# Decay terms through DRAM: thirteen transfers a chunk become eight, and two of the spreads move ahead of the scans

## The chip, the core and the metric

The kernel runs on one core of one Trainium2 chip. A core has five engines that run side by side and meet at semaphores: TensorE (PE; its weight loads are shown apart, as PEld), VectorE (DVE), ScalarE (ACT), GpSimd (POOL) and SyncE (SP), which issues DMAs. ACT and POOL issue DMAs too. The metric is device time in microseconds of one launch.

## The reference

Three layers follow each other on a hidden state of 8 sequences x 1024 tokens x 256, in float32: half a step of a mixture of 8 experts, a "memory" layer, and half a step of the experts again. The change lies in the memory layer:

```python
x = x + 0.5 * ffn(layernorm(x), gate_w, w1, w2)
x = x + attn(layernorm(x), ...)
x = x + 0.5 * ffn(layernorm(x), gate_w, w1, w2)
```

The memory of a sequence is two 64x64 matrices W1, W2 with a momentum S beside them. The tokens go in chunks of 128. The gradient g of a chunk's tokens is taken at the state with which the chunk began, clipped by its norm, and then the state runs token by token:

```python
alpha = (sigmoid(hidden @ aW.T + ab) * 0.1).mean(-1)
eta = (sigmoid(hidden @ eW.T + eb) * 0.9 + 0.05).mean(-1)
theta = (softplus(hidden @ tW.T + tb) * LR).mean(-1)

def step(carry, xs):                      # one token
    Sm, Wm = carry
    gt, et, tt, at = xs
    Sm = et[:, None] * Sm - tt[:, None] * gt
    Wm = (1.0 - at[:, None]) * Wm + Sm
    return ((Sm, Wm), Wm)
```

Each token's output is read from the state after that token: h = silu(q W1), then h W2, an output projection, a norm and a gate.

The kernel does not run this recurrence token by token. With a = 1 - alpha, the state after token t is a sum of three parts: the old W times A(t), the old S times B(t), and the chunk's gradients, each with a weight C(t, s). A is the running product of a, M the running product of eta, and B(t) = a(t) B(t-1) + M(t). C is a 128x128 matrix for each sequence. These are the decay terms that the change is about.

## The kernel before

The 8 sequences are worked on together, chunk by chunk (`NC` = 8 chunks of `P` = 128 tokens, `B` = 8 sequences in `NP` = 4 pairs; of a pair, one sequence lies on partitions 0 to 63 and the other on 64 to 127). The class `Memory` has one small method for each step of a chunk.

The order of the work is written out by hand. `ORDER` (line 1233) is a list of words, and `attention` (line 1248) goes through it once per turn. A word such as `spread` calls that step for the chunk of this turn; `abh1-1` calls `abh` with n=1 for the chunk before, `load1+1` for the chunk after. A step that yields is taken up again at its next word. So each turn mixes steps of up to five chunks, and every engine runs its instructions in the order in which the words issue them. Pools and semaphores are handled by a tile framework: a step that needs another engine's result waits for it in its engine's own queue, and what is behind it there waits too.

The steps around the change, with their lines:

- `ae`, `aem` (693, 708): PE and ACT compute the means. `sig` then holds four rows of 512 numbers: a and eta of sequences 0 to 3 on partitions 0 and 32, of sequences 4 to 7 on partitions 64 and 96.
- `few` (718): four DMAs on SP's queue bring those rows into the small tile `few`, 8 partitions (one for a sequence) x 5 rows x 128: a in row 3, eta in row 4.
- `prods` (732): three scans on DVE over `few`: A into row 0, M into row 2, B into row 1. In the trace all scans have the helper's line, L730.
- `cut` (738): a memset on POOL sets the first token of a and eta to zero, in the small tile, after the scans. `abh1-1` comes next on POOL.
- `spread` (741): on SP, `few` is written to a DRAM tile `kept`; then eta and a go to all 128 partitions (each 128 x 1024 numbers), A and B to `ab`, and the last M to `last`, in six smaller transfers.
- `lt` (756) and `ct` (760): two large scans on DVE, 128 x 1024, over eta and over a. The zero in each sequence's first token is what separates the 8 sequences of one scan. `lt` writes its result over eta. `ends` (765) copies last columns, on POOL.
- `kept` and `past` (796, 788): small copies on POOL for the convolution. (The word `kept` in the order is this step, not the DRAM tile.)
- `abq` (874), `old` (971) and `abh` (1070): POOL multiplies q, the old state and h by A and B. `state` (1001) is the DVE addition that gives the next chunk's state, in the trace L1006.
- `std`, `logits` (1169, 1184): the router of the next layer; POOL's L107 to L112 end in `r_b`, which DVE's L1205 multiplies.
- `xr`, `load` (1100, 658): ACT issues loads of 512 KB each for the residual and for the next chunks.

On SP the thirteen transfers of a chunk are the only ones in this layer, apart from the stores of the last chunk.

Of the kernel before, what the change touches and what calls it, by code (L numbers as in the profile page):

```python
# [10 lines left out]
F32 = mybir.dt.float32  # L11
I32 = mybir.dt.int32
AF = mybir.ActivationFunctionType
ALU = mybir.AluOpType
# [4 lines left out]
P = 128  # L19
B, S, H = 8, 1024, 256  # L20
NT = B * S
NI = NT // P
D = 64
NC = S // P
NP = 4
# [7 lines left out]
class Shared:  # L33
# [95 lines left out]
    def choose(self, pool, dl, mask, ranked=None, cut=lambda ap: ap):  # L129

        nc = self.nc
        n = dl.shape[2]
        full = [P, E, n]
        top = pool.tile([P, 2, n], F32, tag="top", name="top", bufs=1)
        if ranked is None:
            ranked = pool.tile(full, F32, tag="ranked", name="ranked", bufs=1)
        by_e = lambda ap: ap.rearrange("p e i -> p i e")
        nc.vector.tensor_reduce(top[:, 0, :], by_e(dl), AX.X, ALU.max)
        nc.vector.tensor_tensor(dl, dl, top[:, 0:1, :].to_broadcast(full), ALU.subtract)

        nc.vector.scalar_tensor_tensor(
            ranked, dl, -(2.0**-25), self.rank.to_broadcast(full), ALU.is_ge, ALU.mult
        )
        nc.vector.tensor_reduce(top[:, 1, :], by_e(ranked), AX.X, ALU.max)
        first = cut(top[:, 1:2, :])
        nc.vector.tensor_tensor(mask, cut(ranked), first.to_broadcast(list(mask.shape)), ALU.is_equal)


class Slots:
# [37 lines left out]
    def spread(self, _):  # L187

        nc = self.sh.nc
        t_ps = self.pp.tile([P, 512], F32, tag="t", name="t_ps")  # L190
        nc.tensor.transpose(t_ps[:NI, :P], self.by_row, self.sh.ident)
        g = self.pool.tile([NI, P], F32, name="gates")
        nc.scalar.activation(g, t_ps[:NI, :P], AF.Copy, scale=0.5 * 16.0)
        self.gate = self.dr.tile([NT, 1], F32, name="gate_d")
        nc.sync.dma_start(self.gate.rearrange("(i p) o -> i (p o)", p=P), g)
# [310 lines left out]
class Memory:  # L506
# [123 lines left out]
    def new(self, name, shape, **kw):  # L630
        return self.pool.tile(list(shape), F32, tag=name, name=name, **kw)
# [85 lines left out]

    def few(self, c, u, _):

        u.few = self.new("few", (B, 5, P), bufs=1)  # L720
        for h in range(2):
            for n in range(2):
                row = D * h + 32 * n
                self.nc.sync.dma_start(
                    u.few[NP * h : NP * (h + 1), 3 + n, :],
                    u.sig[row : row + 1, 0, :].rearrange("n (j t) -> n j t", j=NP),
                )

    def scan(self, out, m, x, at):
        self.nc.vector.tensor_tensor_scan(out, m, x, at, ALU.mult, ALU.add)  # L730

    def prods(self, c, u, _):
        f = u.few
        self.scan(f[:, 0, :], f[:, 3, :], self.zero, 1.0)
        self.scan(f[:, 2, :], f[:, 4, :], self.zero, 1.0)
        self.scan(f[:, 1, :], f[:, 3, :], f[:, 2, :], 0.0)

    def cut(self, c, u, _):
        self.nc.gpsimd.memset(u.few[:, 3:5, 0:1], 0.0)

    def spread(self, c, u, _):

        nc, new = self.nc, self.new
        kept = self.dram.tile([B, 5, P], F32, tag="kept", name="kept")
        nc.sync.dma_start(kept, u.few)
        u.a, u.eta = new("a", (P, B, P), bufs=1), new("eta", (P, B, P), bufs=1)
        for t, n in ((u.eta, 4), (u.a, 3)):
            nc.sync.dma_start(t, kept[:, n, :].partition_broadcast(P))
        u.ab, u.last = new("ab", (P, 2, NP, P)), new("last", (P, NP, 1))
        for r in range(2):  # L750
            of = kept.rearrange("(p r) n t -> r n p t", r=2)[r]
            for n in range(2):
                nc.sync.dma_start(u.ab[self.half[r], n], of[n].partition_broadcast(D))
            nc.sync.dma_start(u.last[self.half[r]], of[2][:, P - 1 : P].partition_broadcast(D))

    def lt(self, c, u, _):
        flat = lambda ap: ap.rearrange("p b t -> p (b t)")
# [115 lines left out]

    def abq(self, c, u, n):
        self.once(u, "abq", lambda: self.new("abq", (P, 2, NP, P), bufs=1))
        self.nc.gpsimd.tensor_tensor(u.abq[:, n], u.kv[2], u.ab[:, n], ALU.mult)  # L876

# [91 lines left out]
    def old(self, c, u, n):  # L971

        if c + 1 == NC:
            return
        g, st = self.nc.gpsimd, u.st
        at = lambda ap: ap.unsqueeze(3).to_broadcast([P, NP, 2, D])
        self.once(u, "go", lambda: self.new("go", (P, NP, 2, 2, D), bufs=1))
        if n == 0:
            g.tensor_tensor(u.go[:, :, :, 0], st[:, :, :, 0], at(u.ab[:, 0, :, P - 1 : P]), ALU.mult)
        if n == 1:  # L980
            g.tensor_tensor(u.go[:, :, :, 1], st[:, :, :, 1], at(u.ab[:, 1, :, P - 1 : P]), ALU.mult)
        if n == 2:
            g.tensor_tensor(u.go[:, :, :, 0], u.go[:, :, :, 0], u.go[:, :, :, 1], ALU.add)
        if n == 3:
            g.tensor_tensor(u.go[:, :, :, 1], st[:, :, :, 1], at(u.last), ALU.mult)
# [83 lines left out]

    def abh(self, c, u, n):  # L1070
        self.once(u, "abh", lambda: self.new("abh", (P, 2, NP, P), bufs=1))
        self.nc.gpsimd.tensor_tensor(u.abh[:, n], u.hq, u.ab[:, n], ALU.mult)

    def hh(self, c, u, _):
        hh = self.two()
# [160 lines left out]
turn3 turn1 add1-2 load1+1 back_turn0-2 turn2 clip-1 clip-1 lx1+1 turn3 turn2 ae0 back_turn1-2 ae0  # L1236
lx0+1 ae1 lo0-2 old1-1 lo1-2 back_turn0-2 back_turn1-2 ae1 old2-1 old3-1 proj0 clip-1 load0+2 gc0-1
std0-2 gc1-1 aem logits0-2 lx2+1 proj0 proj0 aem logits0-2 hq-1 lx3+1 tap0 tap1 step1-1 logits0-2
few tap2 logits0-2 norm+1 hq-1 hq-1 proj1 step0-1 xr0-1 proj1 prods cut abh1-1 wide1-2 proj1 theta
state-1 wide1-2 tap3 hh-1 proj2 rms1-2 theta tap4 hh-1 xo2-2 abh0-1 theta xn0+1 proj2 zk add2-2  # L1240
proj2 xo3-2 tap5 rh-1 add3-2 zk rows1 soft tap6 rows1 zk softplus lo2-2 pred rows0 lo3-2 pred
back_turn2-2 back_turn2-2 spread tap7 back_turn3-2 rts-1 back_turn3-2 rts-1 ds pred std1-2 tap8
logits1-2 rows0 logits1-2 by_out-1 kept lt logits1-2 ksq sq1 logits1-2 choose1-2 thm pred thm wide0-1 back
past+1 xn1+1 ds by_out-1 abq1 back qk wide0-1 ct back mq0 xn2+1 gate0-1 sq1 store0-2
"""

# [95 lines left out]
```

## Time and profile before

| | us |
|---|---|
| median of three runs | 820.86 (817.55 to 821.42) |
| the profiled execution | 818.81 |
| its span, first to last instruction | 817.0 |
| PE busy | 748.8 (92%) |
| DVE busy | 453.9 (56%) |
| POOL busy | 471.0 (58%) |
| ACT busy | 347.1 (42%) |
| mean granted TensorE clock | 0.948 |

The memory layer lies at about 240 to 580 us; the small scans of its eight chunks begin at 246, 278, 319, 365, 412, 458, 508 and 554 us. Chunks are numbered from 0 here. Ahead of it and behind it are the two expert layers, bound by PE and weights.

In lists in order of time each line gives the start in us, the duration in us, the engine, the source line, the operation, what it writes from what it reads, and in brackets how long the engine had been idle and what ended that. In lists of waits, a line gives who waited, for whom, the total in us, how many times, and the longest. "PEld" is a weight load; it runs ahead of its matmul. A span on POOL includes time in which the operation was held up.

### The profile page before, as it was taken

How to read it: one execution, taken by the hardware profiler on the slowest of the kernel's cores; microseconds unless marked ns; L12 is line 12 of the kernel's file. 1: busy time of each engine (PE TensorE's matmuls, PEld its weight loads, DVE VectorE, ACT ScalarE, POOL GpSimd, SP SyncE). 2: the span in 40 equal slices, each digit the busy share in tenths (PEclk: the TensorE clock that was granted, in tenths of full speed). 3: DMA queues.
4: the chain of work that ended last, by engine and by line, in shares of the span. 5: the costliest groups of instructions: out<-in, count | busy, mean ns of one | idle time of the engine just before them, and what ended most of it. 6: DMA issues, size and time to landing. Idle time of an engine off the chain costs nothing. (4 is left out here: it accounts for less than half of the span.)

```text
span 817.0 us, 13755 instructions
## 1 busy us (share of the span) xinstructions
PE 748.8 (92%) x5256; PEld 544.1 (67%) x5256; DVE 453.9 (56%) x939; ACT 347.1 (42%) x738; POOL 471.0 (58%) x610
## 2 busy tenths in 40 slices
PE   7989999999478999899999999899975899999996
PEld 5657777777336585767767575666763577777775
DVE  7763332220418988788888868978743624322310
ACT  5411222222057676767676655766332122222221
POOL 6626445431234788888888878877754254444411
PEclk9989999999867999999999979999797799999999
DMA  9995445440213334433544532434425724444410
GB/s 299 370 386 166 136 145 168 151 141 16 94 51 80 111 73 125 123 117 79 181 106 155 131 104 80 91 123 99 130 74 183 245 73 139 139 145 139 152 63 18
DMA packets 110945, 110.40 MB, mean 135 GB/s; under 512 B 12384, under 2 KB 103904, under 8 KB 110880
## 3 DMA queue, kind: packets, MB, share of 16 engines
q1 hardware_dynamic: 73312, 66.50, 27.3%
q10 hardware_dynamic: 31680, 31.46, 12.3%
q0 software_dynamic: 5888, 11.57, 4.5%
q8 instruction: 41, 0.67, 0.3%
q14 instruction: 24, 0.20, 0.1%
HBM read 78.80 MB, written 30.64 MB: 134 GB/s over the span
## 5 line engine op out<-in xcount | busy, mean ns | idle before, releaser
L371 ACT ACTIVATE hT<-ph 128x320 f32<-128x320 f32 x128 | 55.9, 437 | 221.9 <-PE ph L364 221.9
L364 PE MATMUL ph<-xT,w1t 128*128 128x320 f32 x512 | 146.0, 438 | 0.9 <-ACT xT L318 0.9
L364 PEld LDWEIGHTS ph<-xT,w1t 128*128 128x128 f32 x512 | 94.7, 190 | 40.6 <-issue 2.7
L392 DVE SCALAR_TENSOR_TENSOR xo<-py,gate,xg 128x256 f32<-128x256 f32 x32 | 15.5, 484 | 186.9 <-PE py L385 186.9
L385 PE MATMUL py<-w2t,hT 128*128 128x256 f32 x512 | 114.6, 382 | 0.0
L385 PEld LDWEIGHTS py<-w2t,hT 128*128 128x128 f32 x512 | 96.1, 190 | 13.7
L287 POOL DMA_INDIRECT gate<-gate_d,get x48 | 45.3, 943 | 39.0 <-DMA gate_d<-gates 25.0
L1111 PE MATMUL pre<-wg,xT 128*128 128x256 f32 x256 | 61.6, 401 | 2.2 <-DVE m L870 2.2
L775 PE MATMUL pre<-xT,w 128*64 128x512 f32 x256 | 61.4, 603 | 0.5 <-ACT kk L807 0.5
L1111 PEld LDWEIGHTS pre<-wg,xT 128*128 128x128 f32 x256 | 50.8, 201 | 11.0 <-DVE m L870 2.7
L1155 POOL TENSOR_TENSOR xo<-xo,xr 128x512 f32<-128x512 f32 x32 | 42.9, 1353 | 20.3 <-DVE xo L1149 20.0
L395 POOL DMA_INDIRECT out<-xo,put x16 | 16.0, 1003 | 54.7 <-DVE xo L392 52.1
L395 POOL DMA_INDIRECT x<-xo,put x16 | 16.0, 1002 | 52.3 <-DVE xo L392 44.4
L678 ACT ACTIVATE xt<-xt,ln_nm,lx_t 128x256 f32<-128x256 f32 x64 | 34.4, 593 | 24.4 <-POOL ln_nm L673 24.4
L1149 DVE SCALAR_TENSOR_TENSOR xo<-tail,rs,gate 128x256 f32<-128x256 f32 x64 | 27.1, 477 | 25.2 <-DMA out<-xo 9.4
L964 DVE TENSOR_TENSOR gc<-ehd,c 128x1536 f32<-128x1536 f32 x16 | 40.0, 2539 | 0.3
L775 PEld LDWEIGHTS pre<-xT,w 128*64 128x64 f32 x256 | 15.8, 136 | 30.4 <-issue 22.4
L685 PE MATMUL pre<-ident,xt 128*128 128x128 f32 x128 | 21.0, 298 | 14.4 <-ACT xt L678 13.0
L876 POOL TENSOR_TENSOR abq<-qq,ab 128x512 f32<-128x512 f32 x16 | 32.8, 2051 | 1.8 <-DMA ab<-kept 1.8
L698 PE MATMUL pre<-xT,w 128*128 128x512 f32 x64 | 32.1, 631 | 0.0
L408 PE MATMUL py<-w2t,hT 128*64 128x128 f32 x512 | 31.5, 276 | 0.0
L276 POOL DMA_INDIRECT xg<-x,get x24 | 23.4, 973 | 13.9 <-DVE get L240 6.8
(254 smaller groups left out, 1593.4 us busy)
## 6 DMA issues: line engine op xcount, KB each, us to landing
w1t<-w_in SPq DMA_DIRECT2D x16, 1024.0 KB
w2t<-w_in SPq DMA_DIRECT2D x16, 1024.0 KB
xt<-hidden_in SPq DMA_DIRECT2D x16, 512.0 KB
x<-xt SPq DMA_DIRECT2D x16, 512.0 KB
xt<-x ACTq DMA_DIRECT2D x16, 512.0 KB
xr<-x ACTq DMA_DIRECT2D x16, 512.0 KB
x<-xo ACTq DMA_DIRECT2D x14, 512.0 KB
out<-xo ACTq DMA_DIRECT2D x14, 512.0 KB
```

The costliest lines, as they stand in the source:

```text
L287: nc.gpsimd.indirect_dma_start(out=gate[:, s : s + 1], out_offset=None, in_=slots.gate, in_offset=bass.IndirectOffsetOnAxis(ap=slots.get[: ...
L364: nc.tensor.matmul(ph[:, :CAP], lhsT=a[:, c, f * P : (f + 1) * P], rhs=at[:, c, :], start=(c == 0), stop=(c == 1),)
L371: nc.scalar.activation(hT[:, f, :], ph[:, :CAP], AF.Relu)
L385: nc.tensor.matmul(py[:, :H], lhsT=hT[:, f, s * P : (s + 1) * P], rhs=b[:, f, :], start=(f == 0), stop=(f == FC - 1),)
L395: nc.gpsimd.indirect_dma_start(out=dst, out_offset=bass.IndirectOffsetOnAxis(ap=slots.put[:, e, s : s + 1], axis=0), in_=xo[:, s, :], in_o ...
L678: self.nc.scalar.activation(x, x, AF.Identity, bias=u.nm[:, j : j + 1], scale=u.r16[:, j : j + 1])
L698: self.nc.tensor.matmul(ps, lhsT=self.w3[:, k, 4 * D : 6 * D], rhs=u.xT[:, k, h * 512 : (h + 1) * 512], start=(k == 0), stop=(k == 1),)
L775: self.nc.tensor.matmul(ps[self.half[r], :], lhsT=self.w3[:, k, f * D : (f + 1) * D], rhs=u.xT[:, k].rearrange("h (p r t) -> h p r t", p=N ...
L876: self.nc.gpsimd.tensor_tensor(u.abq[:, n], u.kv[2], u.ab[:, n], ALU.mult)
L964: self.nc.vector.tensor_tensor(u.gc[:, layer], g.unsqueeze(2).to_broadcast([P, B, 3, D]), u.c3.rearrange("s n j -> s j n").unsqueeze(3).to ...
L1111: self.nc.tensor.matmul(ps[:, q * H : (q + 1) * H], lhsT=u.xT[:, k, j * P : (j + 1) * P], rhs=self.wg[:, k, :], start=(k == 0), stop=(k == 1),
L1155: self.nc.gpsimd.tensor_tensor(u.xo[h][:, two], u.xo[h][:, two], u.xr[h][:, two], ALU.add)
```

## The change

The decay rows go to DRAM first, straight from `sig`, in one transfer of 4 x 512. From there two transfers fill rows 3 and 4 of `few`, and eta and a are spread to 128 partitions at once, before the scans. After the scans only what they made leaves `few`: its rows are so arranged that the last M, A and B are 257 neighbouring numbers of each sequence. They go to a second DRAM tile in one transfer and to `mab` in two. The zero of the first token is now set in the large tiles eta and a, by two memsets in each chunk, and the word `cut` moves in the order from behind `prods` to between `kept` and `lt`. `u.ab` and `u.last` become slices of `mab`, so that A and B have a row step of 257 numbers.

```diff
     def few(self, c, u, _):
+        nc = self.nc
+        kept = self.dram.tile([4, NP * P], F32, tag="kept", name="kept")
+        nc.sync.dma_start(kept, u.sig[0:P:32, 0, :])
+        by_half = kept.rearrange("(h n) x -> n h x", n=2)
         u.few = self.new("few", (B, 5, P), bufs=1)
         for h in range(2):
-            for n in range(2):
-                row = D * h + 32 * n
-                self.nc.sync.dma_start(
-                    u.few[NP * h : NP * (h + 1), 3 + n, :],
-                    u.sig[row : row + 1, 0, :].rearrange("n (j t) -> n j t", j=NP),
-                )
+            nc.sync.dma_start(
+                u.few[NP * h : NP * (h + 1), 3:5, :], by_half[:, h, :].rearrange("n (j t) -> j n t", j=NP)
+            )
+        u.a, u.eta = self.new("a", (P, B, P), bufs=1), self.new("eta", (P, B, P), bufs=1)
+        for to, n in ((u.eta, 1), (u.a, 0)):
+            nc.sync.dma_start(to.rearrange("p (h j) t -> p h (j t)", h=2), by_half[n].partition_broadcast(P))
...
     def prods(self, c, u, _):
         f = u.few
-        self.scan(f[:, 0, :], f[:, 3, :], self.zero, 1.0)
-        self.scan(f[:, 2, :], f[:, 4, :], self.zero, 1.0)
-        self.scan(f[:, 1, :], f[:, 3, :], f[:, 2, :], 0.0)
+        self.scan(f[:, 1, :], f[:, 3, :], self.zero, 1.0)
+        self.scan(f[:, 0, :], f[:, 4, :], self.zero, 1.0)
+        self.scan(f[:, 2, :], f[:, 3, :], f[:, 0, :], 0.0)
+
+    def spread(self, c, u, _):
+        ends = self.dram.tile([B, 2 * P + 1], F32, tag="ends_d", name="ends_d")
+        self.nc.sync.dma_start(ends, u.few.rearrange("b n t -> b (n t)")[:, P - 1 : 3 * P])
+        u.mab = self.new("mab", (P, NP, 2 * P + 1))
+        for r in range(2):
+            of = ends.rearrange("(p r) x -> r p x", r=2)[r]
+            self.nc.sync.dma_start(u.mab[self.half[r]], of.partition_broadcast(D))
+        u.last = u.mab[:, :, 0:1]
+        u.ab = [u.mab[:, :, P * n + 1 : P * (n + 1) + 1] for n in range(2)]

     def cut(self, c, u, _):
-        self.nc.gpsimd.memset(u.few[:, 3:5, 0:1], 0.0)
-
-    def spread(self, c, u, _):
-        nc, new = self.nc, self.new
-        kept = self.dram.tile([B, 5, P], F32, tag="kept", name="kept")
-        nc.sync.dma_start(kept, u.few)
-        u.a, u.eta = new("a", (P, B, P), bufs=1), new("eta", (P, B, P), bufs=1)
-        for t, n in ((u.eta, 4), (u.a, 3)):
-            nc.sync.dma_start(t, kept[:, n, :].partition_broadcast(P))
-        u.ab, u.last = new("ab", (P, 2, NP, P)), new("last", (P, NP, 1))
-        for r in range(2):
-            of = kept.rearrange("(p r) n t -> r n p t", r=2)[r]
-            for n in range(2):
-                nc.sync.dma_start(u.ab[self.half[r], n], of[n].partition_broadcast(D))
-            nc.sync.dma_start(u.last[self.half[r]], of[2][:, P - 1 : P].partition_broadcast(D))
+        for t in (u.eta, u.a):
+            self.nc.gpsimd.memset(t[:, :, 0:1], 0.0)
...
 ORDER
-few tap2 logits0-2 norm+1 hq-1 hq-1 proj1 step0-1 xr0-1 proj1 prods cut abh1-1 wide1-2 proj1 theta
+few tap2 logits0-2 norm+1 hq-1 hq-1 proj1 step0-1 xr0-1 proj1 prods abh1-1 wide1-2 proj1 theta
...
-logits1-2 rows0 logits1-2 by_out-1 kept lt logits1-2 ksq sq1 logits1-2 choose1-2 thm pred thm wide0-1 back
+logits1-2 rows0 logits1-2 by_out-1 kept cut lt logits1-2 ksq sq1 logits1-2 choose1-2 thm pred thm wide0-1 back
```

In `abq`, `abh` and `old`, `u.ab[:, n]` becomes `u.ab[n]`; nothing else changes in them.

More of the change, by code (lines that the diff above doesn't have):

```diff
@@ L875, in abq @@
         self.once(u, "abq", lambda: self.new("abq", (P, 2, NP, P), bufs=1))
-        self.nc.gpsimd.tensor_tensor(u.abq[:, n], u.kv[2], u.ab[:, n], ALU.mult)
+        self.nc.gpsimd.tensor_tensor(u.abq[:, n], u.kv[2], u.ab[n], ALU.mult)
     def by_row(self, lhsT, rhs):
@@ L978, in old @@
         if n == 0:
-            g.tensor_tensor(u.go[:, :, :, 0], st[:, :, :, 0], at(u.ab[:, 0, :, P - 1 : P]), ALU.mult)
+            g.tensor_tensor(u.go[:, :, :, 0], st[:, :, :, 0], at(u.ab[0][:, :, P - 1 : P]), ALU.mult)
         if n == 1:
-            g.tensor_tensor(u.go[:, :, :, 1], st[:, :, :, 1], at(u.ab[:, 1, :, P - 1 : P]), ALU.mult)
+            g.tensor_tensor(u.go[:, :, :, 1], st[:, :, :, 1], at(u.ab[1][:, :, P - 1 : P]), ALU.mult)
         if n == 2:
@@ L1071, in abh @@
         self.once(u, "abh", lambda: self.new("abh", (P, 2, NP, P), bufs=1))
-        self.nc.gpsimd.tensor_tensor(u.abh[:, n], u.hq, u.ab[:, n], ALU.mult)
+        self.nc.gpsimd.tensor_tensor(u.abh[:, n], u.hq, u.ab[n], ALU.mult)
     def hh(self, c, u, _):
```

## The prediction

> **What bounds the kernel now.** The page comes first: span 817.0 us, PE busy 92%, and the code of the change runs in the middle, the attention, about 240 to 580 us. The chain that ended last covers only the last microseconds and says nothing of it. So I read, in this order, the windows of the eight chunks, PE's waits, and one steady chunk in order of time on SP, DVE and POOL.
>
> Windows by stage (columns: busy us and instruction count of PE, PEld, DVE, ACT, POOL, then granted clock, DMA share, GB/s):
>
> ```profile
> 315.00:361.00 46.00, 43.76 (x414) 30.91 (x412) 39.27 (x63) 31.46 (x67) 38.98 (x45) 1.00 0.45 127
> 407.00:453.00 46.00, 43.55 (x410) 30.70 (x408) 39.09 (x62) 31.39 (x67) 39.52 (x48) 1.00 0.47 127
> ```
>
> PE is idle 2 to 2.5 us of a chunk's 46. PE takes its instructions in order, so what makes it wait longer lengthens the chunk. PE's waits of the whole run name the places:
>
> ```profile
> PE core L896 <- DVE ehd L911: 6.7, 7, 1.3
> PE tail L1127 <- DVE dl_b L1205: 4.5, 7, 1.0
> PE core L1079 <- DVE st L1006: 0.9, 1, 0.9
> ```
>
> Every chunk PE waits about 0.95 us for L911 and 0.58 for L1205. L1079 waits once, but PEld lists 6.7 us in 7 times for the same L1006, so PE has no slack there either. All three stand behind work that the change touches. DVE and POOL, chunk 4, around the small scans:
>
> ```profile
> 409.11 0.68 DVE L1068 TENSOR_TENSOR hq<-core,hq 128x512 f32<-128x512 f32 x1
> 412.01 0.73 DVE L730 TENSOR_TENSOR_SCAN few<-few,zero 8x128 f32<-8x128 f32 x2 [2.22 <-DMA few<-sig]
> 413.12 1.19 DVE L1006 TENSOR_TENSOR st<-core,go 128x1024 f32<-128x1024 f32 x1
> ...
> 411.68 0.25 POOL L673 TENSOR_SCALAR ln_nm<-ln_nm 128x8 f32<-128x8 f32 x1
> 413.25 0.09 POOL L739 MEMSET few<- 8x2 f32 x1 [1.32 <-DVE few L730]
> 413.31 1.27 POOL L1072 TENSOR_TENSOR abh<-hq,ab 128x512 f32<-128x512 f32 x1
> ```
>
> DVE waits for the DMA few<-sig, then is busy without a gap from 412.01 to L911 (421.44); PE's L896 follows at 422.17. So the landing of `few` sets PE's clockwork. The same two engines around the large scan `lt`, chunk 3:
>
> ```profile
> 377.87 0.74 DVE L811 SCALAR_TENSOR_TENSOR qq<-raw,cw,qq 128x512 f32<-128x512 f32 x1
> 378.53 2.28 DVE L730 TENSOR_TENSOR_SCAN eta<-eta,diag 128x1024 f32<-128x1024 f32 x1
> 382.66 0.19 DVE L1205 TENSOR_TENSOR dl_b<-tail,r_b 128x32 f32<-128x32 f32 x1 [1.85 <-POOL r_b L112]
> 383.36 3.08 DVE L730 TENSOR_TENSOR_SCAN ct<-a,eta 128x1024 f32<-128x1024 f32 x1
> ...
> 377.97 2.84 POOL L108 TENSOR_TENSOR lo_t<-lo_st 128x4 f32<-128x4 f32 x1
> 380.77 0.20 POOL L109 TENSOR_TENSOR lo_t<-lo_t 128x4 f32<-128x4 f32 x1
> 382.58 0.21 POOL L798 COPY past<-raw 128x36 f32<-128x36 f32 x1
> 383.03 1.27 POOL L918 TENSOR_TENSOR ds<-sg,ds 128x512 f32<-128x512 f32 x1
> ```
>
> Two things to see. A 128x4 POOL operation that takes 0.20 elsewhere (L109) takes 2.84 and ends as `lt` ends (380.81); and `ct` takes 3.08 where it starts inside L918. DVE operations that read two SBUF operands and POOL operations that read SBUF hold each other up, and the one that started first finishes first.
>
> **The change, part by part.** The sum is against the profiled execution, 818.81 us (span 817.0), which lies 2.05 under the median 820.86 of the three runs.
>
> *1. One DMA hop more before the small scans.* Before: four issues few<-sig, SP 407.27 to 409.83. After: one issue kept<-sig, a wait for its landing, two issues few<-kept, then scans. The nearest row for the hop is kept<-few: from its issue at 413.37 to the next issue at 414.92 it takes 1.55 (2.09 in the last chunk). So few's second issue starts about 408.9 to 409.4 plus 0.64, against 409.25 for today's fourth. What decides is the xr load, 512 KB on ACT's queue: in the DMA view its packets run from 408.95 to 411.3, and of today's four few transfers one lands before it and three with its last packets; DVE starts 0.7 later. The new ones should also land as it ends: +0.2 (bounds 0 and +2.9, the latter if kept itself lands only behind the load). Chunk 0 has no such load: today's transfers land as fast as they are issued, scans effectively from 246.5; 243.07 + 1.55 + 1.25 for two issues + 1.75 (issue to scan, there) is 247.6: +1.1. In chunk 1 the load is issued at 273.48, ahead of sig, and today's first few packets come only at its end (276.3). There kept waits for it, and few after it: about 279.8 against 277.8, +2.0.
>
> *2. POOL's wait for the scans goes, and L1072 moves ahead of them.* Today the memset (0.09) waits for the scans, 1.3 us a chunk, and abh (L1072) stands behind it. After, abh follows L673 at once: 411.98 in chunk 4, 319.1 in 2, 365.4 in 3, 458.0 in 5, each for 1.27. The scans, ready 0.0 to 0.35 later (412.2, 319.5, 365.4, 458.3), read two SBUF operands (few and zero) and wait for it. State L1006 then starts about 414.2 in place of 413.12. The tap behind it gains 0.15 (0.90 today, 0.75 free), so L911 and PE's L896 come 0.95 later: four chunks, 3.8. POOL gains nothing, since its next, L1141, waits for ACT's osq until 414.8 either way. In chunks 6 and 7 abh is done before the scans: 0.2 each from part 1. Bounds: 0 (scans on 8 partitions run beside POOL) and 1.3 a chunk.
>
> The Trainium skill (SBUF — State Buffer, Who interferes with whom) says that whichever of the two started first holds the shared port for its whole instruction. The row differs for short reads: in chunk 1 the scans start 0.1 us into L653, a 1.65 us power of 128x8, and run at their usual 0.40. By the page the tap behind the state would also wait for L1142 (1.0 us), and a colliding chunk would cost about 2.6, the sum about 17; I go by the row.
>
> Parts 1 and 2 together: 1.1 + 2.0 + 3.8 + 0.4 = 7.3.
>
> *3. `cut` moves from the small tile to the large ones, ahead of `lt`.* Two POOL memsets of 128x8 (0.11 by L767) per chunk now stand behind L798, and `lt` waits for the first. Behind `lt` on DVE stand L1205, L925 (what PE's L896 of the next step reads) and `ct`; PE's L1127 waits for L1205. If POOL reached L798 when it does today, `lt` would start 383.0 in place of 378.53 and L1205 slip 2.6. But with DVE idle L108 is free at 378.61, L112 and L798 follow in the 2.0 us of today's rows, the memset ends about 380.95, `lt` runs 381.0 to 383.25, L1205 starts 383.22 against 382.66: PE +0.56. POOL's next, L794, is held by `lt`, and `ct` ends 0.35 later, hidden under PE's qk. Chunks 2 to 7: 3.4. Chunk 0 has no L107 to L112 on POOL: L829, L798, cut, then `lt` 254.55 against 253.85, +0.5. Chunk 1: L829 (3.55 today, under `lt`) is free at 289.0, PE's L835 gains 0.5, `lt` comes 1.6 later but m stands within 0.2: -0.3. Sum 3.6; bounds per chunk -0.58 (the PE wait on L1205 vanishes) and +2.6.
>
> *4. What costs nothing.* Five transfers fewer: SP has no issue between 420.3 and 453.3, nothing else is queued on it in the attention. eta and a (1 MB) are issued at 410.1 in place of 414.9, behind few on the same queue; the new ends and M,A,B transfers wait for the scans, then land by about 420; their reader L876 comes at 431: cover 10 us. In chunk 0, where L876 waits 1.8 for ab and PE 0.3 behind it, -0.3. A and B are now read with a row step of 257 elements: DVE's taps on rows of 131 take 0.75 against 0.68 for plain ones, so +0.13 on POOL's 1.27; PE's L1034 starts 0.4 after abh ends, which covers it. At the step from 1.05 to 2.43 that POOL shows between L981 and L985 it would cost 0.9 a chunk, 6 in all; L985 starts inside DVE's gc, which explains it, so 0.
>
> The Trainium skill (DMA: Bandwidth & Descriptors, Rules for kernel authors) counsels merging small transfers, since each pays mostly overhead; by its fit of about 2 us each, five fewer would be 10 us a chunk. The rows show that overhead on SP, where nobody waits, while the one hop that is added has a waiter.
>
> Sum: 7.3 + 3.6 - 0.3 = +10.6, so 829.4 beside 818.81, and 831.5 beside the median.
>
> **Rivals.**
> - *No collision*: the scans start first or run beside abh. For: chunk 3 is a tie. Against: `ct` and L918. Part 2 falls to 0.2 a chunk, 3.0 less: 828.5.
> - *kept caught by the load in every chunk*: its packets would come at about 408.5, only 0.4 before the load's, and a 20 KB write took 0.25. From 0.2 us later on it waits for the load's end, as in chunk 1: scans +2.9 in six chunks in place of 0.95 or 0.2, 13 more: 844.
> - *Covered*: the hop lands with the load, no collision, and POOL reaches cut 0.5 earlier than I think; only chunks 0 and 1 pay, +3 less what the clock gives back (granted 0.90 in 453 to 503, 1.00 in its neighbours): 822 to 824.
> - *Faster*: POOL, rid of its 1.3 us wait, brings r_b early enough that PE's waits for L1205 (4.5) go, from `lt` starting before 380.4 on; with 0.3 of part 4 and few unchanged: 816. Against: my 381.0, from rows of 0.2 to 1.0 each.
>
> **How the numbers follow.** Forecast 45%, no collision 20%, caught 13%, covered 12%, faster 10%. 0.5% is 4.1 us, about what can be told from no change. Slower by more: 45 + 20 + 13 and none of covered, 78%; same: 12%; faster: 10%. The likeliest's own range is 827 to 837; to leave out no more than 2 in 10 it reaches from 820 (most of covered) to 842 (up to the caught case with some chunks spared).
>
> **What would show it.** Part 1: scans start 0 to 0.4 later after sig in chunks 2 to 7, about 2 in chunk 1. Part 2: L1072 right behind L673, the first small scan 1.3 us long or late, L1079 with a PE wait of about 1 in chunks 2 to 5. Part 3: L108 falls from 2.84 to under 1, a DVE wait of 2.4 for POOL before `lt`, PE's wait before L1127 at 1.1. Wrong if the scans start with today's delay after sig, or if `lt` starts before 380.4 in that chunk's time.

## The result and the profile after

The changed kernel takes 832.13 us (median of six runs, 825.34 to 834.73) beside 821.14 for the kernel before (817.55 to 823.48). The ratio is 1.0129, 95% interval 1.0085 to 1.0174: 10.6 us slower, with an interval of 7.0 to 14.3. The prediction was 831.5, 10.6 over the median before. The profiled execution took 833.62 us, its span is 831.8 and its mean granted clock 0.937, against 818.81, 817.0 and 0.948 before. Ratios here and below leave out runs that were more than 1.5% longer than the fastest of the same kernel, which is why a profiled run may lie far from them.

New lines of code push the numbers on: up to three in the changed kernel (the scans are L734, `cut` L757, state L1009, PE's reader of it L1082, `abh` L1075, `dl_b` L1208, PE's reader of that buffer L1130), and by a few more in some experiments.

The waits of PE over the whole run, kernel after (who waits, for whom: us in total, times, longest):

```profile
PE tail L1130 <- DVE dl_b L1208: 7.5, 7, 1.9
PE core L1082 <- DVE st L1009: 6.7, 6, 3.9
PE core L899 <- DVE ehd L914: 6.7, 7, 1.0
```

Before, the same three were 4.5, 0.9 and 6.7. So the wait for `dl_b` grew by 3.0 and that for the state by 5.8; the third stayed. Of the 6.7 for the state, 3.9 is a single wait, in chunk 1. Of the 3.0 for `dl_b`, chunks 2 to 6 give 0.31 each (0.89 in place of 0.58) and chunk 7 gives 1.35. Chunk 4 in order of time, kernel after, SP, then DVE, then POOL:

```profile
418.96 0.53 SPq L722 DMA_DIRECT2D kept<-sig  x1
420.71 0.61 SPq L726 DMA_DIRECT2D few<-kept  x2
...
423.98 1.49 DVE L734 TENSOR_TENSOR_SCAN few<-few,zero 8x128 f32<-8x128 f32 x2 [2.51 <-DMA few<-kept]
425.85 1.19 DVE L1009 TENSOR_TENSOR st<-core,go 128x1024 f32<-128x1024 f32 x1
...
440.00 2.33 DVE L734 TENSOR_TENSOR_SCAN eta<-eta,diag 128x1024 f32<-128x1024 f32 x1 [2.13 <-POOL a L757]
442.25 0.16 DVE L1208 TENSOR_TENSOR dl_b<-tail,r_b 128x32 f32<-128x32 f32 x1
...
423.70 1.19 POOL L1075 TENSOR_TENSOR abh<-hq,mab 128x512 f32<-128x512 f32 x1
437.22 0.71 POOL L108 TENSOR_TENSOR lo_t<-lo_st 128x4 f32<-128x4 f32 x1
439.70 0.21 POOL L801 COPY past<-raw 128x36 f32<-128x36 f32 x1
439.85 0.11 POOL L757 MEMSET eta<- 128x8 f32 x1
440.14 3.25 POOL L921 TENSOR_TENSOR ds<-sg,ds 128x512 f32<-128x512 f32 x1
```

What to see. `abh` starts 0.28 ahead of the scans, and the two scans take 1.49 in place of 0.73: that is the collision. In chunk 5 it is the second scan that `abh` meets, which takes 1.33 in place of 0.39, and in chunk 1 two operations of `abh` lie on both. So chunks 1 to 6 collide in this execution, and the first two scans are lengthened by 5.6 us in all. `lt` waits 2.13 for POOL, 16.0 us behind the scans in place of 13.3. L108 fell from 2.84 to 0.71, since no scan holds it up now; in return `lt` holds up L921, which takes 3.25 in place of 1.27. From kept's issue to few's it is 1.75 (3.35 in chunk 1).

One thing was not in the prediction. Three neighbouring stretches of 3.41 us of the same chunk, kernel after (start:end, us, busy time and count of PE, PEld, DVE, ACT, POOL, granted clock, DMA share, GB/s):

```profile
439.74:443.15 3.41, 2.52 (x22) 1.98 (x19) 3.15 (x4) 2.34 (x6) 3.41 (x5) 1.00 0.00 0
443.16:446.57 3.41, 3.41 (x24) 2.44 (x23) 2.38 (x1) 1.53 (x6) 3.36 (x2) 0.50 0.00 0
446.58:449.98 3.40, 3.40 (x31) 3.06 (x30) 2.48 (x4) 2.17 (x7) 2.35 (x3) 1.00 0.62 208
```

The first holds PE's wait ahead of L1130 (0.89 in this chunk, 0.58 before); in the one right behind it TensorE has half its clock. Such a stretch stands behind L1130 in each of chunks 3 to 7, and they lie 47.79 us apart, 14 times 3.41, like the chunks. Chunk 2 has one of 10.24. Before, three of the chunks 2 to 7 had one, of 3.41, 10.24 and 10.24. Chunks 3, 4 and 5 of the kernel before, from sig to sig, have one of 3.41, none and one of 10.24:

```profile
360.69:407.25 46.56, 45.03 (x410) 32.10 (x408) 39.11 (x62) 31.39 (x68) 39.60 (x49) 0.96 0.45 126
407.25:453.24 45.99, 43.54 (x410) 30.69 (x408) 39.08 (x62) 31.38 (x67) 39.51 (x48) 1.00 0.47 127
453.24:503.40 50.16, 48.32 (x410) 34.36 (x408) 38.69 (x62) 31.51 (x67) 40.89 (x54) 0.90 0.37 107
```

The same 410 matmuls keep PE busy for 43.5 us at full clock, 45.0 with the short stretch and 48.3 with the long one, and the chunk is longer by some 0.7 and 4.3. So chunks are best compared at the same granted clock.

### The profile page after: what moved, and what is told of

It is laid out like the page before. It is cut to its first block, busy times and chain, and to the rows that moved or that the text cites. A ratio compares the mean times of both kernels' runs of the same rounds, so it can differ in the third digit from the quotient of the medians.

```text
span 831.8 us, 13693 instructions
## 1 busy us (share of the span) xinstructions
PE 754.6 (91%) x5256; PEld 547.6 (66%) x5256; DVE 456.1 (55%) x939; ACT 347.2 (42%) x738; POOL 468.6 (56%) x618
## 5 line engine op out<-in xcount | busy, mean ns | idle before, releaser
L778 PE MATMUL pre<-xT,w 128*64 128x512 f32 x256 | 63.2, 618 | 0.5 <-ACT kk L810 0.5
L1114 PE MATMUL pre<-wg,xT 128*128 128x256 f32 x256 | 59.5, 392 | 0.7 <-DVE m L873 0.7
L1158 POOL TENSOR_TENSOR xo<-xo,xr 128x512 f32<-128x512 f32 x32 | 42.9, 1353 | 22.4 <-DVE xo L1152 20.5
L879 POOL TENSOR_TENSOR abq<-qq,mab 128x512 f32<-128x512 f32 x16 | 34.8, 2180 | 0.0
L1130 PE MATMUL tail<-wo,rts 64*128 64x256 f32 x128 | 26.6, 444 | 7.5 <-DVE dl_b L1208 7.5
L807 ACT COPY raw<-pre 128x512 f32<-128x512 f32 x24 | 14.1, 587 | 43.5 <-PE pre L778 41.0
L408 PE MATMUL py<-w2t,hT 128*64 128x128 f32 x512 | 31.5, 276 | 0.0
```

The lines of the kernel that those rows point to most:

```text
L408: nc.tensor.matmul(py[h * D : (h + 1) * D, :P], lhsT=hT[:, f, 2 * P :], rhs=b[:, f, h * P : (h + 1) * P], start=(f == 0), stop=(f == FC - ...
L778: self.nc.tensor.matmul(ps[self.half[r], :], lhsT=self.w3[:, k, f * D : (f + 1) * D], rhs=u.xT[:, k].rearrange("h (p r t) -> h p r t", p=N ...
L879: self.nc.gpsimd.tensor_tensor(u.abq[:, n], u.kv[2], u.ab[n], ALU.mult)
L1114: self.nc.tensor.matmul(ps[:, q * H : (q + 1) * H], lhsT=u.xT[:, k, j * P : (j + 1) * P], rhs=self.wg[:, k, :], start=(k == 0), stop=(k == 1),
L1158: self.nc.gpsimd.tensor_tensor(u.xo[h][:, two], u.xo[h][:, two], u.xr[h][:, two], ALU.add)
```

## The experiments

All ratios are to the kernel before, run beside the changed one on the same chip. The experiments ran on four chips, on which its own median was 819.4 (`hold`, the early `cut`, both, the late xr load), 835.9 (the first two kernels without the hop, `lt` moved), 834.3 (the third kernel without the hop, the fill) and 818.8 (the hop alone): chips differ by more than the change is worth, so only ratios are compared between them.

**The collision and the place of `cut`.** First, `abh` is held behind the scans again by a memset of two rows that nobody reads afterwards (of the order's long lines only the words around a change are shown, here and below):

```diff
+    def hold(self, c, u, _):
+        self.nc.gpsimd.memset(u.few[:, 3:5, 0:1], 0.0)
...
-proj1 prods abh1-1
+proj1 prods hold abh1-1
```

> The changed kernel with POOL held back again: a memset of the first tokens in rows 3 and 4 of the small tile (which nothing reads any more) stands behind the scans and ahead of abh, as the old cut did. Everything else as changed. Theory (three terms: hop, collision, cut): abh no longer runs into the small scans; the first small scan takes 0.41 in every chunk (in the changed kernel it took 0.81 to 1.43 in five chunks, 3.7 us more in all), and the time falls by 3 to 4 us, to about 828.5. Rival 'the hop alone' (the whole loss is the additional transfer ahead of the scans, what POOL does is hidden): no change, 832, or a little slower for the wait put back. Rival 'clock' (the loss is the granted clock, 0.937 against 0.948): no change.

Measured: 826.17, ratio 1.0079 (1.0044 to 1.0113). DVE and POOL in order of time, chunk 4 of this kernel:

```profile
420.99 0.73 DVE L734 TENSOR_TENSOR_SCAN few<-few,zero 8x128 f32<-8x128 f32 x2 [3.47 <-DMA few<-kept]
...
422.23 0.09 POOL L755 MEMSET few<- 8x2 f32 x1 [2.55 <-DVE few L734]
422.29 1.18 POOL L1078 TENSOR_TENSOR abh<-hq,mab 128x512 f32<-128x512 f32 x1
```

The scans are back at 0.73 in all chunks. Between 315 and 600 us PE's waits for the state fall from 2.8 us in 5 times to 1.0 in one. The ratio falls by 0.0050, some 4 us, where 3.8 had been predicted and a little over 3 was expected of this run; the intervals of the two ratios overlap, so the size is uncertain by as much again.

Then `cut` is issued earlier on POOL, alone and together with `hold`:

```diff
-by_out-1 kept cut lt
+by_out-1 kept lt
...
-xo2-2 abh0-1 theta
+xo2-2 abh0-1 cut theta
```

> The changed kernel with the word cut moved in the order from between kept and lt to behind abh0-1: POOL sets the zeros of eta and a some 13 us before lt asks for them. Theory: DVE's waits for POOL before lt (15.6 us in 8 times) go, its waits for r_b ahead of L1208 come back (1.2 now, 12.3 before), PE's wait ahead of L1130 falls from about 1.1 to 0.6 a chunk, and the time falls by 3 to 4 us, to about 828.5. Rival 'the hop alone': no change, 832. Rival 'clock': no change.

> Both edits together: of the change only the transfers are left, the POOL steps stand as in the kernel before. Theory: the two gains add, 7 us, and 825 is left, that is 3.5 to 4 us over the kernel before, of which chunk 0 has 0.5 to 1 and chunk 1 about 2. Rival 'the hop alone': 832. If the terms overlap (the same PE wait paid twice): 828.

Measured: 828.21, ratio 1.0115 (1.0081 to 1.0149), and 826.63, ratio 1.0067 (1.0033 to 1.0101). The waits of PE over the whole run, `cut` moved alone:

```profile
PE core L1082 <- DVE st L1009: 6.7, 5, 3.9
...
PE tail L1130 <- DVE dl_b L1208: 4.6, 7, 1.1
```

The wait for `dl_b` is back at the size it had before the change, 2.9 us less, and yet the time falls by only about 1 us, with an uncertainty of 4 to 5. So the step does what it was said to do to the waits; its price measures about 1 us, and the 3.6 that was predicted lies within the uncertainty. Both together leave +0.67%, more than the 825 that was expected: of the three terms the hop alone stays in that kernel, and it was priced at 3.5 us. The second pair of kernels says the same as the first: `hold` takes the ratio from 1.0115 to 1.0067 where `cut` is early, 0.0048, and the early `cut` from 1.0079 to 1.0067 where `abh` is held, 0.0012.

What no pair of ratios resolves can be read within one execution. Chunks 5 and 6 of the kernel with `cut` early, from sig to sig:

```profile
467.51:513.34 45.83, 43.54 (x410) 30.70 (x408) 38.96 (x62) 31.42 (x67) 37.07 (x42) 1.00 0.39 116
513.34:560.17 46.83, 43.61 (x410) 30.67 (x408) 37.99 (x54) 31.41 (x67) 39.06 (x49) 1.00 0.32 103
```

Chunk 5 has no collision there (first scan 0.41), chunk 6 has one (1.31). Both have the full clock, and the second takes 1.00 longer. Chunks 2 and 3, with first scans of 1.24 and 1.42, take 46.35 and 46.83, also at full clock. So a colliding chunk costs 0.5 to 1.0, about the 0.95 of the prediction.

**What the landing of `few` is worth.** In the kernel before, the xr load is issued behind the state:

```diff
-step0-1 xr0-1 proj1
+step0-1 proj1
-state-1 wide1-2 tap3
+state-1 xr0-1 wide1-2 tap3
```

> The kernel before with one word moved: xr0-1, ACT's load of 512 KB, issued behind the state instead of just behind sig. It asks whether the transfers into the small tile wait for that load. Theory: they land as they are issued, the first scan starts 3.2 to 3.7 us after sig instead of 4.2 to 4.9, the state and PE's waits for L1006 and L911 come earlier, and the time falls by 3 to 6 us, to 815 to 818. Rival (the transfers cost that long by themselves): scans as before, 821. Rival (PE is the bound, the scans do not set it): scans earlier, time 821.

Measured: 820.67, ratio 0.9982 (0.9949 to 1.0015). The waits of DVE in the memory layer of this kernel:

```profile
DVE m L1084 <- PE core L1079: 8.6, 7, 3.0
DVE few L730 <- DMA few<-sig: 6.4, 14, 1.3
```

The scans now start 3.04 to 3.13 after sig in chunks 2 to 7, against 4.39 to 4.89 before; so `few` does wait for the end of that load there. But the time does not change beyond the noise, and the two chunks at full clock take 45.77 and 46.04, as before (45.77 to 45.99). DVE, earlier with the state, then waits longer for L1079 (1.7 us in two waits before). The prediction had read "the landing of `few` sets PE's clockwork"; when it lands earlier by 1.3 to 1.8 us, nothing is gained.

**The hop taken out.** The rows come straight from sig again, and kept, eta and a follow them. Alone, and with `hold` and the early `cut`:

```diff
+        u.few = self.new("few", (B, 5, P), bufs=1)
+        for h in range(2):
+            for n in range(2):
+                row = D * h + 32 * n
+                nc.sync.dma_start(
+                    u.few[NP * h : NP * (h + 1), 3 + n, :],
+                    u.sig[row : row + 1, 0, :].rearrange("n (j t) -> n j t", j=NP),
+                )
         kept = self.dram.tile([4, NP * P], F32, tag="kept", name="kept")
         nc.sync.dma_start(kept, u.sig[0:P:32, 0, :])
         by_half = kept.rearrange("(h n) x -> n h x", n=2)
-        u.few = self.new("few", (B, 5, P), bufs=1)
-        for h in range(2):
-            nc.sync.dma_start(
-                u.few[NP * h : NP * (h + 1), 3:5, :], by_half[:, h, :].rearrange("n (j t) -> j n t", j=NP)
-            )
```

> Of the changed kernel only the hop is undone: four transfers bring the rows straight from sig into few, and kept, eta and a follow them; cut and L1075 stay as changed. Theory (the hop costs what the run with both other parts undone left, +5.9 by the means): about 826 to 827 beside 831.5, ratio to the kernel before 1.008; the small scans start 4.2 to 4.6 us after sig in chunks 2 to 7 and 4.2 in chunk 1 in place of 5.2. The prediction's sizes (3.5 for the hop): 828. Rival (what that run left is not the hop but the earlier spread of eta and a or the merged tiles): 831 to 832, no gain.

> Hop, collision and cut ahead of lt all undone; what stays of the change is that eta and a leave for their tiles before the scans, and M, A and B go in one piece. Theory (the three terms are all there is): 819 to 821, ratio 1.000 (0.997 to 1.003). Rival (early spread of eta and a, or the row step of A and B, has its own price): it stays at 825 to 827, ratio 1.006 or more. Second rival (fewer transfers are worth something once the hop is gone): under 817.

Measured: ratio 1.0051 (1.0003 to 1.0099) and 1.0043 (1.0009 to 1.0076). Without the hop 0.78% of the 1.29% is gone, though with an interval as wide as that: the rival of no gain is out, but the theory and the prediction's sizes both lie within it. In chunks 0 and 1 its periods from sig to sig are 30.68 and 41.27, as before the change (30.64 and 41.28). The second is 0.43% where 0 was expected. POOL at the start of chunk 0 of that kernel, in order of time:

```profile
259.27 0.12 POOL L763 MEMSET eta<- 128x8 f32 x1 [4.65 <-DMA eta<-kept]
261.11 0.11 POOL L763 MEMSET a<- 128x8 f32 x1 [1.71 <-DMA a<-kept]
261.17 1.97 POOL L838 TENSOR_TENSOR sp<-pos,sp 128x512 f32<-128x512 f32 x1
```

The early `cut` waits there for a landing, and the sum L838 behind it, for which PE waits, is held up with it. So one more kernel keeps the late place in chunk 0 alone:

```diff
+    def cut(self, c, u, late):
+        if late == (c == 0):
...
-xo2-2 abh0-1 cut theta
+xo2-2 abh0-1 cut0 theta
...
-by_out-1 kept lt
+by_out-1 kept cut1 lt
```

> As the run with hop, collision and cut ahead of lt all undone, but in chunk 0 cut stays behind kept, since there POOL's early cut waited 6 us for the landing of eta and a and held up the sum L838 that TensorE's L844 waits for (1.7). Theory (the 0.43% that was left is this wait of chunk 0, 2.7 us): chunk 0 is back at 30.6 us, ratio 1.000 (0.997 to 1.003). Rival (0.43% is a price of the early spread or of the merged tiles in every chunk): ratio 1.003 or more with chunk 0 at 30.6.

Measured: ratio 0.9982 (0.9946 to 1.0019). With hop, collision and late `cut` gone, the change costs nothing that can be measured, and gains nothing: no version here is faster than the kernel before. But the reason given for the 0.43% was not shown. In this kernel's profiled execution (842.85 us, one of its longest) PE's wait for the sum fell from 2.3 to 0.6 as expected, while chunk 0 still takes 33.24, not 30.6: PE now waits 1.8 there for L935. Chunk 0 comes in two forms, 30.6 to 31.5 and 33.2 to 34.0, in kernels with and without the hop. One profile says nothing of what it costs, and the two ratios are from different chips with intervals that touch.

**The hop alone, in the kernel before.**

```diff
+        hop = self.dram.tile([4, NP * P], F32, tag="hop", name="hop")
+        nc.sync.dma_start(hop, u.sig[0:P:32, 0, :])
+        by_half = hop.rearrange("(h n) x -> n h x", n=2)
         u.few = self.new("few", (B, 5, P), bufs=1)
         for h in range(2):
-            for n in range(2):
-                row = D * h + 32 * n
-                self.nc.sync.dma_start(
-                    u.few[NP * h : NP * (h + 1), 3 + n, :],
-                    u.sig[row : row + 1, 0, :].rearrange("n (j t) -> n j t", j=NP),
-                )
+            nc.sync.dma_start(
+                u.few[NP * h : NP * (h + 1), 3:5, :], by_half[:, h, :].rearrange("n (j t) -> j n t", j=NP)
+            )
```

> The kernel before with the hop alone: the rows go from sig to DRAM in one transfer and from there to few in two; everything behind it, cut and L1072 too, as before. Theory (the hop is the largest part, as two differences of earlier runs have it: 7.0 between the runs without the other two parts, 6.4 between the changed kernel and the one without the hop): 5 to 8 us, ratio 1.006 to 1.010, with PE's wait for L1006 in chunk 1 at 2.0 or more (0.9 before), and the rest through later scans in chunks 2 to 7. The prediction's sizes (1.1 + 2.0 + 0.2 a chunk): 4.3 us at most, ratio 1.004 to 1.005, with the wait of chunk 1 alone longer. Rival (the parts do not add up; the hop by itself is hidden and costs only where L1072 goes ahead of the scans): ratio 1.000 to 1.002.

Measured: 824.64 beside 818.78, ratio 1.0068 (1.0047 to 1.0090), 5.6 us with an interval of 3.8 to 7.4. This is the sharpest of the differences, and it agrees with the 1.0067 of the changed kernel with `hold` and the early `cut`, in which of the three terms only the hop is left. The waits of PE between 240 and 320 us of this kernel, which are chunks 0 and 1:

```profile
PE core L1080 <- DVE st L1007: 2.0, 1, 2.0
...
PE core L887 <- DVE m L1085: 0.9, 1, 0.9
```

The windows of those two chunks, of this kernel:

```profile
241.90:272.82 30.92, 26.68 (x196) 17.33 (x192) 27.50 (x36) 21.69 (x38) 15.67 (x15) 0.89 0.37 87
272.82:317.43 44.61, 40.92 (x366) 29.07 (x368) 36.62 (x57) 28.22 (x55) 33.25 (x42) 0.96 0.32 85
```

Chunk 1 takes 44.61 where the kernel before takes 41.28. The scans start 1.03 later after sig there (5.21 against 4.18), the state's wait grows from 0.9 to 2.0, PE then waits 0.9 for m, which it did not before, and one half-clock stretch of 3.41 falls into the chunk. In chunks 2 to 7 the scans come 0.1 later on average, and the two chunks at full clock take 45.79 and 46.00, against 45.77 to 45.99. So chunk 1 gives some 3.3 of the 5.6. In chunks 2 to 6 the hop costs nothing at full clock; but chunks 3 and 6 of this execution hold a stretch of 10.24 at half clock each and take 49.99 and 49.87, where the kernel before had one such among these. The mean granted clock over these 12 runs is 0.9436, against 0.9492 over 17 runs of the kernel before. That the rest arises there is likely, but one profile does not settle it.

**The wait ahead of L1127 and the clock.** Two ways were tried. The first moves `lt` behind `dl_b` and `e` on DVE, in the kernel before and in the changed one:

```diff
-kept lt logits1-2 ksq sq1 logits1-2 choose1-2 thm pred thm wide0-1
+kept logits1-2 ksq sq1 logits1-2 choose1-2 thm pred lt thm wide0-1
```

> The kernel before with one word moved: lt goes behind dl_b and e on VectorE, so that the two small results that TensorE waits for no longer stand behind a scan of 2.3 us. Theory (that wait before L1127, 0.58 a chunk in seven chunks, lengthens the chunk): it falls to 0.2 or less, 3 to 4 us less, 816 to 817, ratio 0.995 to 0.996; if the clock windows follow such waits, one or two of the half-clock stretches go as well, 0.7 each. Rival (ct, now 2 us later, or the next wait takes the gain): 820 to 822, ratio 1.000 to 1.002, with a wait of m for ct in place of that for dl_b.

> The changed kernel with the same word moved: cut stays where the change put it, but dl_b and e no longer stand behind the scan that waits for it. Theory (the third part costs only through TensorE's wait for dl_b, 0.89 to 1.9 a chunk, and through the half-clock windows right behind it): that wait falls under 0.3, the half-clock window that follows it in chunks 3 to 7 goes, 831.5 becomes 823 to 826, ratio 1.004 to 1.007. Prediction's size alone (0.56 a chunk, no effect on the clock): 828. Rival (the chunk is bound by the scans and by L1082, so this wait only moves): 830 to 832.

Measured: ratio 1.0174 (1.0125 to 1.0222) and 1.0221 (1.0180 to 1.0262): both expectations were missed, and the rival was too mild. The waits of PE in the memory layer, then DVE and PE in order of time in chunk 3, of the kernel before with `lt` late:

```profile
PE pre L1111 <- DVE m L870: 20.4, 7, 3.1
```

```profile
398.04 0.19 DVE L1205 TENSOR_TENSOR dl_b<-tail,r_b 128x32 f32<-128x32 f32 x1 [2.41 <-PE tail L1202]
398.74 2.59 DVE L730 TENSOR_TENSOR_SCAN eta<-eta,diag 128x1024 f32<-128x1024 f32 x1
401.36 3.21 DVE L730 TENSOR_TENSOR_SCAN ct<-a,eta 128x1024 f32<-128x1024 f32 x1
...
405.43 6.85 PE L1111 MATMUL pre<-wg,xT 128*128 128x256 f32 x17 [3.13 <-DVE m L870]
```

The wait for `dl_b` is gone, as meant. But DVE is now idle for 2.41 until PE delivers, time that `lt` used to fill, and `ct` ends so late that PE waits 3 us a chunk for m.

The second leaves the order alone and gives PE matmuls of 128x128 by 256 columns in that wait, whose result nobody uses: two of them in the kernel before, three in the changed one.

```diff
                     u.po[h][r][:, q * H : (q + 1) * H], lhsT=u.rts[part, 2 * h + q, :], rhs=self.wo[part], start=True, stop=True
                 )
+                if h + q + r == 0:
+                    for _ in range(2):
+                        self.nc.tensor.matmul(
+                            u.po[h][r][:, H:], lhsT=self.sh.ident, rhs=self.sh.jrow[:, :H], start=True, stop=True
+                        )
```

> The kernel before, and in the wait ahead of L1127 (0.58 us a chunk) TensorE runs two more matmuls of 128x128 by 256 columns whose result nobody uses, about 0.46 us by the 0.23 of L1111's. Theory (the half-clock windows of the memory layer follow windows that end in this wait): the stretches at half clock that begin about 1 us behind L1127 in three of eight chunks go, mean clock up by 0.004 to 0.010, 3 to 8 us less: 812 to 817 beside 820, ratio 0.990 to 0.997. Rival (the clock does not hang on this wait): ratio 1.000 to 1.003, the same share of chunks with a half-clock stretch, and the mean clock as before.

> The changed kernel with three such matmuls (0.7 us) in the wait ahead of L1130 (0.89 a chunk). Theory (the cut's price is mostly the half-clock window behind that wait): the 3.41-us stretches behind L1130 in chunks 3 to 7 go, 0.7 each and more in the chunk with a stretch of 10.24; 4 to 7 us less than the changed kernel, ratio to the kernel before 1.004 to 1.008 in place of 1.013. Rival (the clock does not hang on it): ratio 1.012 to 1.015.

Measured: ratio 0.9993 (0.9962 to 1.0024) and 1.0124 (1.0077 to 1.0171). The window from 277 to 597 us, which holds chunks 1 to 7, of the kernel before with fill, and of the changed one with fill:

```profile
277.00:597.00 320.00, 308.13 (x2814) 215.91 (x2812) 265.28 (x406) 211.82 (x441) 260.92 (x302) 1.00 0.42 117
```

```profile
277.00:597.00 320.00, 305.01 (x2774) 213.95 (x2772) 262.69 (x394) 207.85 (x434) 251.37 (x305) 1.00 0.37 113
```

Without fill the clock in this stretch is 0.96 and 0.95. So the half-clock stretches of chunks 2 to 7 do hang on that wait: filled, not one is left. That half of the theory stands. The other half, that they make up the cut's price, is not borne out: both expected gains were missed, no gain can be told from zero in either kernel, and with fill in both the changed one is still 1.3% behind. The test is not clean, though. The fill itself takes longer than planned and longer than the waits of 0.58 and 0.89, 1.13 and 1.56 us rather than 0.46 and 0.7. In the profile of the kernel before with fill, the five periods from chunk 2 to chunk 7 add up to 231.6, 2.7 less than the 234.3 before, but chunk 0 takes 34.0 and chunk 1 42.9, 5.0 more. Of the five, the four without a wait for L1119 take 45.91 to 46.06, so at full clock the fill adds 0.1 to 0.2 a chunk. The first fill matmul runs at 304.94, behind chunk 0 (251.2 to 285.2): the 3.4 that chunk 0 lost is no work of the fill. Why the runs as a whole gained nothing is open.

## Why the prediction was right, and where it was off

The sum came out right, 10.6 predicted and 10.6 measured, but its terms were not all of the right size. That the totals agree so closely is luck: the hop was priced some 2 us too low and `cut` by the measured sizes some 2 to 3 too high, which cancel, and the measurement has an interval of 7.0 to 14.3. The runs give the hop alone 5.6 (3.8 to 7.4), and everything but the hop (the changed kernel with the rows straight from sig) 0.51% or 4.3 (0.3 to 8.3). Together that is 9.9. The hop was priced at 3.5 and the rest at 7.1.

- *One DMA hop more*: right in kind, too small in size, and too large in each delay. The scans start 0.54 later in chunk 0 (1.1 predicted), 1.00 in chunk 1 (2.0), and 0.06 on average in chunks 2 to 7 (0.2). One reason is that few's two issues take 0.61 together, not the 1.25 that four transfers of one row had led to. The step that failed is the next one, which took a delay of the scans for a delay of PE. In chunk 1 one microsecond of delay cost 3.3, where a further wait and a half-clock stretch followed; in chunks 2 to 7 a gain of 1.3 to 1.8 us was worth nothing that could be measured, so the landing of `few` does not set PE's pace there.
- *The collision*: shown. `abh` right behind L673, the scans lengthened, PE waiting for the state, 0.3 to 0.9 in chunks 2 to 6 where about 1 in 2 to 5 had been predicted. Chunks 1 to 6 collide in this execution rather than 2 to 5, since it is a tie of some tenths. Holding `abh` back won about 4, uncertain by as much, against 3.8; chunks at the same clock give 0.5 to 1.0 for each collision, against 0.95.
- *`cut` ahead of `lt`*: right in mechanism. DVE's wait of 2.13 for POOL (2.4 predicted), L108 under 1, PE's wait for `dl_b` grown by 3.0 us over the run (3.4 predicted for six chunks), though by 0.31 and not 0.56 in chunks 2 to 6. Taking those waits away again won only about 1 us, resolved neither from zero nor from 3.6. So the term looks too large, and its last step is the doubtful one: that a chunk grows by as much as one wait of PE in it.
- *What costs nothing*: held. With the three terms undone the merged transfers measure 0.9982 (0.9946 to 1.0019). A and B with a row step of 257 take 1.18 on POOL against 1.27; 0.13 more had been estimated.
- *Rivals*: "no collision" and "kept caught by the load" are refuted by the scans' lengths and starts, "faster" by `lt` starting 2.7 later after the scans. "Covered" is refuted by the ratio. In chunk 1, where the prediction let kept wait for the load, it takes 3.35 from kept's issue to few's, against 1.75 in chunk 4.
- *The granted clock* was not in the sum. In chunks 2 to 7 the half-clock stretches follow PE's wait ahead of L1130 (shown by the fill). A chunk that holds one is longer in the same execution, by 0.7 with 3.41 and 4.3 with 10.24; but filling them away won nothing over whole runs, so what they add to the change's price is open.

The Trainium skill (TensorE: Matmul & The Clock Gate, Why this matters for your kernels) has the clock fall after gaps of PE of more than about 3 us. The rows here show it at half behind a stretch of 3.41 us in which PE was busy for 2.52, with a gap of 0.89. So here a much shorter gap was enough.

## What to carry to other kernels

Fewer transfers gained nothing here (0.9982, 0.9946 to 1.0019), where nobody waited for the queue, and the one hop that was added had a waiter. When a wait is removed from an engine, ask what now runs earlier and beside what: a POOL operation that used to stand behind a semaphore came to lie on top of the scans. And price a delay by a run that delays that one thing: neither the length of a wait nor its disappearance told what it was worth. Where the differences are smaller than the noise between runs, compare chunks of one execution at the same granted clock.

## What the runs showed of the hardware

- TensorE's clock went to half in stretches of 3.41 us, or two or three of them in a row, behind waits of 0.58 to 1.93 us ahead of L1127 (by its number in the kernel before), though not behind each of them: of the six waits of 0.58 in the kernel before, three were followed by one. Waits of 0.9 to 1.3 us ahead of L896, which follow other matmuls, were not followed by it in the steady chunks. Matmuls of 128x128 by 256 columns in the wait kept the clock at 1.00 from 277 to 597 us.
- The same kernel before had medians of 818.8, 819.4, 834.3 and 835.9 on four chips: 2% between them, 1.6 times the effect that was studied.
- Two transfers of 4 x 2 rows were issued in 0.61 us, where four of single rows out of sig took 2.55.
